# Graph attention over 16 batches: an output tile of its own for batch 14, one key sum on GpSimd, batch 2's labels loaded once, label counts directly behind an eviction

## The chip, the cores and the metric

The kernel runs on one core of a Trainium2 chip. The metric is the device time of one execution in microseconds. Engines are named as in the profile: PE (TensorE matmul), PEld (its weight load), DVE (VectorE), ACT (ScalarE), POOL (GpSimd), SP (the SyncE queue that issues most DMAs).

## The reference

One layer of relation-aware graph attention, with B = 16 batches, N = 512 nodes of F = 512 features, a conditioning vector of 512, H = 16 heads of 32, and keys taken from the first 20 nodes. There are two directions d (the label tensor as it is, and with its node axes swapped). All in float32.

```python
self_feat = concat([v, where(row_zero, 0, q)]) @ W_self.T + b_self
output = self_feat
for d in range(2):
    A = (adj if d == 0 else swapaxes(adj, 1, 2))[:, :, :20, :]      # 11 labels a pair
    mask = A.sum(-1) > 0 ; bias = A @ w_bias + b_bias
    kv = self_feat[:, :20]
    aff = (self_feat Wq[d] + bq) . (kv Wk[d] + bk) / sqrt(32)       # by head
    w = softmax(where(mask, aff, -9e15) + bias)
    output += (w @ kv) @ Wout[d] + bout[d]                          # by head
return v + relu(output)
```

## The kernel before, in words

The order of all instructions is written out by hand; each engine works through its own list in that order, and waits only where a semaphore asks for it.

**Setup.** Keys for all batches are folded into one matrix per batch, so that scores are one product of a batch's features with its "keys". `keys(runs)` does this in 20 bursts (n = 0 to 19): PE fills two PSUM pairs, ACT and DVE evict one half each (L939, L941), and finished blocks are copied by POOL (L945) and sent to DRAM. Bursts 13 to 19 also carry one block product each of batch 0's self features (`block_product`, L284), in the order 1, 2, 6, 7, 5, 4, 3; products 1, 6, 7 and 4 add up in one PSUM bank, `ps_a`, and DVE reads it after each one (`partial`, L297, two instructions). Label work of batch 0's second half lies in these bursts too: `mask_count` (DVE L332: how many labels a pair has, then POOL L333) at n = 15, `mask_sum` (DVE L338: the bias) at n = 17. Both stand behind the block product's DVE instruction in the burst.

**The loop** runs over b = 0 to 14, each pass mixing scores of batch b (seven score products, L397, by a Winograd-like 2x2 scheme), self features of batch b + 1 (`self_product`, L657), softmax of b (`weigh` L522/L523, `expo` L527, `total` L531/L532, `normal` L536 on POOL, `turn` L544) and output of b - 1 and b - 2 (`attend` L567, `finish` L584, `store` L613). The scheme needs sums of key blocks (`key_sum`, L370) and of feature blocks (`feat_sum`, L377 and L384). Key sum 3 of batch 0 is worked out in place, on DVE, ahead of the loop:

```python
        seed_d(0)
        key_sum(0, 3, nc.vector)
        feat_sum(0, 1, nc.vector)
        feat_sum(0, 2, nc.vector)
```

Its reader is score product 7 of batch 0. That product and product 6 share the PSUM tile `ps_a`, which `lowered` (DVE L502) reads between the two. For later batches key sum 3 is on POOL already, one pass ahead.

**Labels.** `load_adj(b, h, ins, ts)` loads half h of a batch's labels (two slices t of 220 KB each; a new buffer of three is taken when slice 0 is among them). `ins` is an instruction behind which the DMA is put in SP's queue. From batch 3 on the four slices come one by one. For batch 2 the code of pass 0 loads slice 0 of half 0, and pass 1 takes new buffers and loads both halves whole; the first slice is thus loaded twice. The labels are read by `mask_mul` (ACT L327, one instruction a label) and `mask_count`.

**The end.** Behind the loop stands a list for b = 15 and o = b - 1 = 14. Outputs are put together in the tile `outt[...]`, tag "o" of the pool `work`, with one buffer: batch 14's tile is batch 13's, whose last two chunks leave by `store(b - 2, range(2, 4))`. Batch 14's output is written by `relieve` (ACT L594: relu out of PSUM), then `residual` (POOL L599: plus x), or by `finish` (DVE L584: both). The first of them stand in this order, where `seed_out` (ACT L554) puts the self features into the PSUM banks of batch 15's output, which `attend(b, ...)` on PE then adds to:

```python
        for q in (3, 2):
            relieve(o, q)
        seed_out(b, 0)
        seed_out(b, 1)
        residual(o, 3)
        total(b, 0, 1)
        normal(b, 0, 1)
        finish(o, 0)
```

Inputs x of batch b lie in four tiles: tags "x0", "x1", "x2" of the pool `load`, and a late tile for b % 4 == 3. "x0" last holds batch 12, whose last reader is `finish(12, ...)` in pass 14.

Of the kernel before, what the change touches and what calls it, by code (L numbers as in the profile page):

```python
# [7 lines left out]
F32 = mybir.dt.float32  # L8
# [10 lines left out]
def gat_kernel(  # L19
# [669 lines left out]
    with tc.tile_pool(name="setup", bufs=1) as sp, tc.tile_pool(name="ps_acc", bufs=4, space=PSUM) as acc["pool"]:  # L689
# [160 lines left out]
        with tc.tile_pool(name="setup_g", bufs=3) as sg:  # L850
# [39 lines left out]
            def value_pieces():  # L890

                while ended:
                    t, ds, ps = ended.pop()
                    rows = min(P, BM - t * P)
                    v = msk.tile([P, H * S], F32, tag="full", name=f"v{t}{ds[0]}")[:, :F]
                    nc.vector.scalar_tensor_tensor(v, br_sb, 0.5, ps, ALU.mult, ALU.add)
                    for i, d in enumerate(ds):
                        edge = EARLY * NG
                        for n, lo, hi in ((0, 0, edge), (1, edge, rows)) if t == 0 else ((1, 0, rows),):
                            nc.gpsimd.dma_start(  # L900
                                vw_d[n][d, :, bass.ds(t * P + lo - n * edge, hi - lo)].rearrange("c r w -> r c w"),
                                v[bass.ds(i * rows + lo, hi - lo)].rearrange("p (c w) -> p c w", c=C),
                            )
# [4 lines left out]
            def keys(runs):  # L908


                pairs = [ps_s.tile([P, 2, 512], F32, tag=f"s{i}", name=f"ps_g{runs[0]}{i}", bufs=1) for i in range(2)]
                at = 0
                for fc, hg, d, lo, hi in runs:
                    n = (hi - lo) * ND
                    for hl in range(HL):
                        r = bass.ts(hl, DH)
                        nc.tensor.matmul(
                            pairs[hl // 2][:, hl % 2, at : at + n], wq_sb[r, d, hg, bass.ts(fc, P)],
                            khD[r, d * C + hg, lo * ND : hi * ND], start=at == 0, stop=True, skip_group_check=True,
                        )  # L920
                    at += n
                if not units and runs is bursts[-1]:
                    for hl in range(HL):
                        r = bass.ts(hl, DH)
                        nc.tensor.matmul(
                            pairs[hl // 2][:, hl % 2, at:], wq_sb[r, 0, 0, :P], khD[r, 0, : 512 - at],
                            start=False, stop=True, skip_group_check=True,
                        )
                at = 0
                for fc, hg, d, lo, hi in runs:  # L930
                    n = (hi - lo) * ND
                    if (fc, hg) not in stages:
                        stages[fc, hg] = (late if hg == C - 1 else sg).tile([P, B, HL, 2, ND], F32, tag="st", name=f"st{fc}{hg}")
                    st = stages[fc, hg]
                    for half in range(2):
                        to = st[:, lo:hi, bass.ts(half, 2), d].rearrange("p b h m -> p h b m")
                        of = pairs[half][:, :, at : at + n].rearrange("p h (b m) -> p h b m", m=ND)
                        if half == 0:
                            nc.scalar.activation(to, of, AF.Copy, scale=SCALE)  # L939
                        else:  # L940
                            nc.vector.tensor_scalar(to, of, SCALE, None, ALU.mult)  # L941
                    at += n
                    if d == 1 and hi == B:
                        to, of = g0[:, fc, bass.ts(hg, WD // C)], st[:, 0].rearrange("p h d m -> p (h d m)")
                        nc.gpsimd.tensor_copy(to, of)  # L945
                        nc.sync.dma_start(g1_d[C * fc + hg], st[:, 1].rearrange("p h d m -> p (h d m)"))
                        if fc * hg < (C - 1) * (C - 1):
                            nc.sync.dma_start(g_d[C * fc + hg], st[:, 2:])
# [40 lines left out]
            for n, runs in enumerate(bursts):  # L989
                for i in range(len(rest)):  # L990
                    if (i < 1 and n > 0) or any(fc == 0 and (d, hg) == rest[0] for fc, hg, d, _, _ in runs):
                        key_rows(*rest.pop(0))
                if n in (3, 4):
                    values(*steps["v"].pop(0)[1])
                if n == 0:
                    bo_rows = load.tile([P, C, N], F32, tag="x2", name="bo_rows", bufs=1)
                    nc.sync.dma_start(bo_rows[:, :2], bout.partition_broadcast(P))
                keys(runs)
                value_pieces()
                if rest:  # L1000
                    for kind in "mm" if n else ():
                        f, args = steps[kind].pop(0)
                        f(*args)
                    continue
                first = n if first is None else first
                for kind in plan[n - first] if n - first < len(plan) else ():
                    f, args = steps[kind].pop(0)
                    f(*args)
                if n == first:
                    for d in range(2):  # L1010
                        nc.gpsimd.tensor_add(br_sb, br_sb, bo_rows[:, d])
                if n > first:
                    value_pieces()
                if n == 7:
                    mask_mul(0, 0)
                if n == 8:
                    mask_count(0, 0)
                if n == 10:
                    mask_sum(0, 0)
                    load_cq(0)  # L1020
                if n == 7:
                    clear_first()
                if n == 9:
                    row_sums(1)
                    copies = blocks(0)
                if n > 13:
                    spill(1, nc.gpsimd)
                    spill(1)
                if n == 11:
                    new_self(0)  # L1030
                    for i in range(1, 5):
                        x_sum(0, i)
                if 10 < n < 15:
                    mask_spread(0, 0, (n - 11,))
                if n == 14:
                    mask_mul(0, 1)
                if n == 15:
                    mask_count(0, 1)
                if n == 16:
                    gs[0] = g0  # L1040
                    key_sum(0, 1)
                    load_adj(1, 0)
                if n == 17:
                    mask_sum(0, 1)
                if n == 18:
                    mask_spread(0, 1)
                    key_bias(0)
                    load_adj(1, 1)
                    load_cq(1)
# [7 lines left out]
    with tc.manual_schedule():  # L1057
        seed_a(0)
        seed_d(0)
        key_sum(0, 3, nc.vector)  # L1060
        feat_sum(0, 1, nc.vector)
        feat_sum(0, 2, nc.vector)
        for b in range(B - 1):
            one, two, more, further = b > 0, b > 1, b + 1 < B, b + 2 < B

            def at(yes, f, *args):
                if yes:
                    f(*args)
# [9 lines left out]
            if b == 1:  # L1078
                self_join(1, 0, 1)
                feat_sum(1, 1)  # L1080
                feat_sum(1, 2)
                total(0, 1, 0)
                normal(0, 1, 0)
                turn(0, 1, 1)
                for h in range(2):
                    load_adj(2, h)
            for q in range(2):
                at(two, finish, b - 2, q)
            at(two, store, b - 2, range(1))
# [44 lines left out]
            if more:  # L1134
                self_join(b + 1, 0, 0)
                feed_c(b + 1)
                self_sum(b + 1, 3)
                mask_mul(b + 1, 0, range(7 if one else 0, 11))
            total(b, 0, 0)
            at(more, load_keys, b + 1, range(2, 3), done["sum"])  # L1140
# [64 lines left out]
            joined_with(b, "c", 1, 0)  # L1205
            if b == 0:
                load_nz(2, done["mixed"])
            at(further, load_adj, b + 2, 0, done["mixed"], slice(0, 1))
            weigh(b, 1, 0)
            at(one, new_outs, b - 1)  # L1210
            at(one, seed_out, b - 1, 2)
# [31 lines left out]
            if more:  # L1243
                if further:
                    seed_a(b + 1)
                    seed_d(b + 1)
                else:
                    full_block(b + 1, 1, 0)
                    seed_block(b + 1, 0, 0, [pair(f"ps_a{b + 1}", b + 1)])
                    seed_block(b + 1, 1, 0, [pair(f"ps_d{b + 1}", b)])  # L1250
                mask_sum(b + 1, 1)
                at(one and further, load_adj, b + 2, 1, done["masks"], slice(1, 2))
                at(b < B - 2, mask_spread, b + 1, 1)
            if b == 0:
# [24 lines left out]
        turn(o, 0, 1)  # L1279
        seed_block(b, 0, 1, [pair("ps_l", 1)])  # L1280
        new_outs(o, ((accs, "c"),))
        seed_out(o, 0)
        seed_out(o, 1)
        load_values(o)
# [112 lines left out]
```

## Time and profile before

| what | us |
|---|---|
| median of 3 runs | 554.29 (554.29 to 554.86) |
| the profiled execution | 554.31 |
| its span, first to last instruction | 552.5 |
| PE busy | 540.7 (98%) |
| PEld busy | 425.3 (77%) |
| DVE busy | 481.1 (87%) |
| POOL busy | 435.9 (79%) |
| ACT busy | 404.2 (73%) |

All times in the rows below are from the start of the span. A row of the timeline has a start, a length, engine, line, operation, what it writes and reads, and a count of merged instructions; in brackets the idle time before it and what ended it. A row of the chain has a start, a length and what. A row of waits has who waited for whom, then total us, times, longest. A row of the windows has the stretch, its length, and the busy time of PE, PEld, DVE, ACT and POOL with instruction counts, then the granted TensorE clock, DMA share and GB/s.

### The profile page before, as it was taken

The page shows a single profiled execution, that of the slowest core. Times are in us where ns is not written, and L with a number is a line of the kernel's source. Part 1 is how long each engine was busy: PE and PEld are TensorE (multiplying, and loading weights), DVE is VectorE, ACT ScalarE, POOL GpSimd, SP SyncE. Part 2 cuts the span into 40 slices and gives each one's busy share as a digit, 9 for nine tenths or more (in the row PEclk, how much of TensorE's full clock was granted, in tenths as well). Part 3 has the DMA queues.
Part 4 walks back from the last instruction along what each step waited for, and adds up shares of the span by engine and source line. Part 5 has one row for each costly group of instructions (what it writes and reads, how often), then busy time and mean ns, then how long its engine had stood idle before and what let it go on. Part 6 is the DMA issues. An engine that isn't in the chain of part 4 may idle for free.

```text
span 552.5 us, 19630 instructions
## 1 busy us (share of the span) xinstructions
PE 540.7 (98%) x7908; PEld 425.3 (77%) x7908; DVE 481.1 (87%) x709; ACT 404.2 (73%) x1000; POOL 435.9 (79%) x420
## 2 busy tenths in 40 slices
PE   9999999999999999999999999999999999999992
PEld 6544368898888878787888888788888787878881
DVE  0776678898989999999999999999999999999985
ACT  1225345788897979888888888888888887877743
POOL 2637896689979797979797888888888889797565
PEclk9999999999999999999999999999999999999998
DMA  8999999958886878788776758686767677654034
GB/s 298 377 396 361 306 355 350 300 188 260 251 254 192 232 223 226 220 224 228 221 217 200 229 178 240 193 234 192 221 197 234 198 222 211 181 146 141 18 100 153
DMA packets 100674, 126.68 MB, mean 229 GB/s; under 512 B 19608, under 2 KB 68822, under 8 KB 98536
## 3 DMA queue, kind: packets, MB, share of 16 engines
q1 hardware_dynamic: 98840, 122.16, 70.7%
q0 software_dynamic: 1168, 2.23, 1.7%
q8 instruction: 62, 1.02, 0.8%
q10 hardware_dynamic: 576, 1.05, 0.5%
q14 instruction: 28, 0.23, 0.2%
HBM read 86.45 MB, written 40.24 MB: 229 GB/s over the span
## 4 chain that ended last, share of the span: by engine, by line
PE 87%; DVE 5%; ACT 2%; POOL 2%; DMA 1%; issue 1%; DVEq 0%; SPq 0%; ACTq 0%; POOLq 0%
PE ps_f L657 29%; PE ps_a L397 21%; PE ps_c L397 11%; PE ps_d L397 5%; PE ps_o_f L567 5%; PE ps_v L883 3%; PE ps_k L825 3%; PE ps_kv L767 1%; PE ps_a L284 1%; PE ps_o_c L567 1%; DMA out_T<-o 1%; POOL w L536 1%; PE ps_c L284 1%; POOL full L440 1%; DMA adj<-in_adj 1%
## 5 line engine op out<-in xcount | busy, mean ns | idle before, releaser
L327 ACT ACTIVATE prod<-adj,wb_sb 128x80 f32<-128x80 int32 x330 | 116.0, 430 | 1.0 <-DMA adj<-in_adj 1.0
L536 POOL TENSOR_TENSOR w<-w,sm 128x640 f32<-128x640 f32 x63 | 80.2, 1273 | 32.6 <-DVE sm L532 31.4
L657 PE MATMUL ps_f<-t,ws_s 128*64 128x246 f32 x720 | 80.0, 370 | 0.0
L657 PEld LDWEIGHTS ps_f<-t,ws_s 128*64 128x64 f32 x720 | 52.2, 136 | 18.5
L527 ACT ACTIVATE w<-w 128x640 f32<-128x640 f32 x60 | 43.9, 732 | 19.3 <-DVE w L523 19.3
L544 DVE STREAM_TRANSPOSE wt<-w 128x640 f32<-128x640 f32 x63 | 52.5, 833 | 2.5 <-POOL w L536 2.4
L657 PE MATMUL ps_f<-x,ws_v 128*64 128x246 f32 x480 | 52.4, 371 | 0.0
L531 DVE TENSOR_REDUCE sm<-w 128x32 f32<-128x640 f32 x63 | 51.1, 811 | 1.0 <-ACT w L527 0.9
L522 DVE TENSOR_REDUCE ps_d<-w 128x32 f32<-128x640 f32 x59 | 48.7, 826 | 1.8 <-ACT ps_d L431 0.2
L523 DVE TENSOR_TENSOR w<-w,ps_d 128x640 f32<-128x640 f32 x59 | 48.4, 821 | 2.0
L657 PEld LDWEIGHTS ps_f<-x,ws_v 128*64 128x64 f32 x480 | 34.7, 137 | 13.0
L370 POOL TENSOR_TENSOR k<-g,k 128x608 f32<-128x608 f32 x30 | 44.6, 1486 | 0.0
L397 PEld LDWEIGHTS ps_a<-g,sf 128*64 128x64 f32 x544 | 34.3, 137 | 5.9 <-issue 5.8
L338 DVE TENSOR_REDUCE add<-prod 128x80 f32<-128x960 f32 x32 | 36.7, 1147 | 2.4 <-POOL prod L333 1.5
L397 PE MATMUL ps_a<-g,sf 128*64 128x152 f32 x544 | 38.6, 295 | 0.0
L397 PE MATMUL ps_d<-g,sf 128*64 128x152 f32 x544 | 37.9, 293 | 0.0
L567 PE MATMUL ps_o_f<-wt,vd 32*32 32x256 f32 (+3 forms) x708 | 37.7, 383 | 0.0
L567 PE MATMUL ps_o_c<-wt,vd 32*32 32x256 f32 (+1 forms) x720 | 36.8, 386 | 0.0
L346 ACT COPY both<-add 64x80 f32<-64x80 f32 x128 | 32.6, 254 | 5.7 <-DVE add L338 4.6
L672 POOL TENSOR_TENSOR t<-x,t 128x492 f32<-128x492 f32 x30 | 34.9, 1163 | 1.2
L397 PEld LDWEIGHTS ps_d<-g,sf 128*64 128x64 f32 x544 | 35.3, 137 | 0.2 <-ACT sf L675 0.2
L333 POOL TENSOR_SCALAR prod<-cond 128x80 f32<-128x80 f32 x32 | 18.0, 563 | 21.6 <-DVE cond L332 20.2
(299 smaller groups left out, 1438.7 us busy)
## 6 DMA issues: line engine op xcount, KB each, us to landing
g<-g_d SPq DMA_DIRECT2D x60, 304.0 KB, 3.6
g_d<-st SPq DMA_DIRECT2D x16, 1064.0 KB, 8.6
out_T<-o SPq DMA_DIRECT2D x63, 256.0 KB, 2.6
x<-in_xT SPq DMA_DIRECT2D x56, 256.0 KB, 4.1
xn<-in_xn SPq DMA_DIRECT2D x48, 256.0 KB
adj<-in_adj SPq DMA_DIRECT2D x53, 220.0 KB, 2.8
vd<-bd_d SPq DMA_DIRECT2D x64, 64.0 KB, 2.3
nz<-nz_d SPq DMA_DIRECT2D x14, 256.0 KB, 4.4
```

Of the source, the lines that this page charges most:

```text
L327: nc.scalar.activation(p[:, :, l], a[:, :, l], AF.Identity, scale=wb_sb[:, l : l + 1])
L338: done["masks"] = nc.vector.tensor_reduce(add, prods.pop((b, h)), AX.X, ALU.add)
L370: done["ksum"] = engine.tensor_sub(to, one, two)
L397: nc.tensor.matmul(slot(g)[bass.ts(p, P // 2), : HL * S].rearrange("p (h m) -> p h m", m=NG)[:, :, 1:], of(k)[:, bass.ds(first + g * P // ...
L522: nc.vector.tensor_reduce(mx, f, AX.X, ALU.max)
L523: done["weigh"] = (engine or nc.vector).tensor_sub(f, f, mx.unsqueeze(2).to_broadcast([P, per, NG]))
L527: done["exp"] = nc.scalar.activation(t, t, AF.Exp)
L531: nc.vector.tensor_reduce(sm, heads(weighs[b, c, l]), AX.X, ALU.add)
L536: done["normal"] = nc.gpsimd.tensor_mul(f, f, smalls.pop((b, c, l)).unsqueeze(2).to_broadcast([P, per, NG]))
L544: done["turn"] = nc.vector.transpose(wts[b][:, c, l], weighs.pop((b, c, l)).rearrange("p g w -> p (g w)"))
L567: nc.tensor.matmul(outsum[b][a][bass.ds(at // 2 * DH, n * DH), bass.ds(c * N // 2 + lo * P, (hi - lo) * P)].rearrange("p (n r) -> p n r", ...
L657: nc.tensor.matmul(parts[b][n in (2, 3, 5)][bass.ts(a, P // 2), bass.ts(i, HN)], lhs, x[:, k], start=False, stop=k == 1, skip_group_check= ...
```

## The change

Four edits. (1) Before batch 14's output is seeded, `outt[14]` is given a tile of its own, tag "x0" of the pool `load`. (2) Key sum 3 of batch 0 leaves its place ahead of the loop on DVE; it is issued on POOL in pass 0, behind `self_sum(1, 3)`. (3) Pass 0 loads both slices of half 0 of batch 2's labels at the place where it loaded one, and half 1 behind `mask_sum(1, 1)`; the two loads of pass 1 go. (4) In the setup, `mask_count(0, 1)` and `mask_sum(0, 1)` move up in their bursts, from the end to directly behind `keys(runs)`.

```diff
                 keys(runs)
+                if n == 15:
+                    mask_count(0, 1)
+                if n == 17:
+                    mask_sum(0, 1)
                 value_pieces()
...
-                if n == 15:
-                    mask_count(0, 1)
...
-                if n == 17:
-                    mask_sum(0, 1)
...
         seed_d(0)
-        key_sum(0, 3, nc.vector)
         feat_sum(0, 1, nc.vector)
...
                 turn(0, 1, 1)
-                for h in range(2):
-                    load_adj(2, h)
...
                 self_sum(b + 1, 3)
+                at(b == 0, key_sum, 0, 3)
                 mask_mul(b + 1, 0, range(7 if one else 0, 11))
...
-            at(further, load_adj, b + 2, 0, done["mixed"], slice(0, 1))
+            at(further, load_adj, b + 2, 0, done["mixed"], slice(0, 1 + (b == 0)))
...
                 mask_sum(b + 1, 1)
+                at(b == 0, load_adj, 2, 1, done["masks"])
...
         new_outs(o, ((accs, "c"),))
+        outt[o] = load.tile([P, C, N], F32, tag="x0", name=f"o{o}", bufs=1)
         seed_out(o, 0)
```

## The prediction

> **What bounds the kernel now.** I read the windows by stage first, then PE's waits, then the timeline at each wait. Times are in us. The span, and the stages:
>
> ```profile
> span 552.5 us, 19630 instructions
> ```
>
> ```profile
> 92.00:103.10 11.10, 10.74 (x140) 8.93 (x136) 10.74 (x12) 6.02 (x14) 8.73 (x8) 1.00 0.91 295
> 103.10:130.00 26.90, 26.55 (x338) 24.03 (x340) 23.47 (x33) 24.14 (x66) 21.87 (x21) 1.00 0.79 259
> ...
> 147.00:490.00 343.00, 343.00 (x5171) 282.72 (x5166) 322.46 (x456) 290.50 (x731) 290.54 (x265) 1.00 0.73 214
> ...
> 535.00:552.50 17.50, 7.82 (x233) 5.98 (x208) 9.40 (x21) 5.98 (x13) 7.81 (x8) 0.87 0.35 128
> ```
>
> The second number is the length, the third PE's busy time. The long middle has no idle PE at all: 343.00 of 343.00. There a microsecond taken from any other engine is worth nothing, and a microsecond gained before it is carried through whole, because PE sets the pace. Only three places are left: some 0.36 before 103.1, 0.35 before 130, and the last 17.5, of which PE works 7.82. PE's waits name them:
>
> ```profile
> PE ps_o_s L567 <- ACT o L594: 2.7, 1, 2.7
> PE ps_o_s L567 <- DVE wt L481: 1.4, 1, 1.4
> ...
> PE ps_a L397 <- DVE w L502: 0.7, 2, 0.4
> ```
>
> The 2.7 is in the end, the 0.7 are the two idle bits of the first passes. Three of the four edits stand at these waits, the fourth stands in the setup. The profiled execution took 554.31, its span 552.5, so 1.81 lie around the span; its time is 0.02 above the median of 554.29, and I work from it. A change of 0.2%, 1.1 us, is about what a measurement of this kernel can tell from none.
>
> **Edit 1, the output tile.** It removes a wait and adds no instruction. The place:
>
> ```profile
> 534.89 0.38 PE L567 MATMUL ps_o_s<-wt,vd 32*32 32x256 f32 x2
> 535.20 4.36 PE L397 MATMUL ps_e<-g,sf 128*64 128x152 f32 x64
> 542.25 0.40 PE L567 MATMUL ps_o_s<-wt,vd 32*32 32x256 f32 x2 [2.70 <-ACT o L594]
> ```
>
> ```profile
> 537.95 1.09 ACT L594 ACTIVATE o<-ps_o_s 128x512 f32<-128x512 f32 x2 [2.57 <-DMA out_T<-o]
> 538.92 1.76 ACT L554 ACTIVATE ps_o_s<-sf 128x512 f32<-128x512 f32 x3
> ```
>
> ```profile
> 537.87 0.69 DVE L584 SCALAR_TENSOR_TENSOR o<-ps_o_c,x 128x512 f32<-128x512 f32 x1 [1.25 <-DMA out_T<-o]
> ```
>
> ```profile
> 533.44 4.26 DMA out_T<-o
> ...
> 538.62 1.26 POOL o L599
> 539.89 1.24 POOL w L536
> 541.15 0.84 DVE wt L544
> ```
>
> PE ends batch 14's `attend` at 534.89 + 0.38 = 535.27. ACT could then take the first `relieve`, but the tile still holds batch 13's chunks, whose store runs from 533.44 to 537.70. ACT idles 2.57, DVE 1.25. Behind the `relieve` everything follows without a gap: ACT 0.6, POOL's `residual` 1.26, POOL's `normal` 1.24, DVE's `turn` 0.84, which ends at 541.99, and PE starts at 542.25. "x0" was last read in pass 14, long ago, so the wait goes and this chain starts 2.57 earlier. What is late next: PE itself, which works on the `ps_e` scores until 535.20 + 4.36 = 539.56; PE would start `attend` at 542.25 - 2.57 = 539.68, just behind. On ACT the three seeds follow the two `relieve`: from 535.38, 1.09 and 1.76 end at 538.2, in time. DVE's `finish` gains its 1.25, starting at 536.62, and its next reader of `ps_e` waits for PE instead. From the `turn` to the last store each step waits for the one before, so the end moves by the same amount; the 1.4 behind L481 stays. Between the bounds 1.25 (DVE's share alone) and 2.69 (542.25 - 539.56, where PE is the limit) I take ACT's row: **-2.57**.
>
> **Edit 2, the key sum.**
>
> ```profile
> 92.06 3.15 DVE L370 TENSOR_TENSOR g<-g 128x608 f32<-128x608 f32 x1
> ...
> 97.72 0.81 DVE L508 TENSOR_TENSOR w<-ps_d,w 128x640 f32<-128x640 f32 x1
> ```
>
> ```profile
> 92.06 1.49 POOL L370 TENSOR_TENSOR k<-g,k 128x608 f32<-128x608 f32 x1
> ...
> 98.89 1.23 POOL L672 TENSOR_TENSOR t<-x 128x492 f32<-128x492 f32 x1
> 102.41 1.27 POOL L536 TENSOR_TENSOR w<-w,sm 128x640 f32<-128x640 f32 x1 [2.28 <-DVE sm L532]
> ```
>
> ```profile
> 100.90 1.83 PE L657 MATMUL ps_f<-t,ws_s 128*64 128x246 f32 x16
> 103.09 2.29 PE L397 MATMUL ps_a<-g,f 128*64 128x152 f32 x32 [0.35 <-DVE w L502]
> ```
>
> ```profile
> 107.44 1.68 PE ps_f L657 x16
> ```
>
> DVE loses an instruction of 3.15; POOL gets one of 1.49, the length of the same operation in its own row. It comes behind the row at 98.89, so from 100.12 to 101.61, into the 2.28 that POOL idles there; `normal` at 102.41 stays clear of it even if it is 0.8 sooner. No DMA moves with it. Its reader, score product 7, now waits for POOL, and at 101.61 PE is still on the run begun at 100.90. That run hands over after 1.68 (the chain's row for such a run), at 102.58; product 7 started at 103.09 because L502 was late. So PE has 0.51 to win and no more, as soon as DVE is 0.5 earlier at L502. Between 0 and -0.51 I take **-0.51**.
>
> How much earlier is DVE? From 92.06 + 3.15 = 95.21 to 97.72 lie the two feature sums, 2.5. Without the key sum they could end at 94.7, 3 sooner. But the same operation takes DVE 3.15 and POOL 1.49, beside each other from 92.06 on. The Trainium skill ("SBUF — State Buffer", Who interferes with whom) has it that a DVE instruction with two SBUF inputs and a GpSimd one that reads SBUF exclude each other for the whole instruction. By that rule, with which the two rows agree, most of the 3.15 was waiting for POOL, and a feature sum will wait in its place. If the first of them then ends only where the key sum ends now, at 95.21, DVE wins one feature sum of two, half of 2.5, instead of 3. L502, which now ends just ahead of 103.09, would still end near 101.9 and ahead of 102.58: the sum is the same by both, with some 0.7 in hand instead of 2.
>
> **Edit 3, the labels.**
>
> ```profile
> 115.50 0.93 SPq L123 DMA_DIRECT2D adj<-in_adj  x1
> ...
> 120.67 0.96 SPq L123 DMA_DIRECT2D adj<-in_adj  x2
> ```
>
> ```profile
> 124.20 1.43 ACT L327 ACTIVATE prod<-adj,wb_sb 128x80 f32<-128x80 int32 x4 [1.04 <-DMA adj<-in_adj]
> ```
>
> ```profile
> 127.90 0.82 DVE L531 TENSOR_REDUCE sm<-w 128x32 f32<-128x640 f32 x1 [0.35 <-ACT w L527]
> ```
>
> ```profile
> 127.72 1.86 PE L657 MATMUL ps_f<-t,ws_s 128*64 128x246 f32 x16
> 129.93 2.29 PE L397 MATMUL ps_a<-g,f 128*64 128x152 f32 x32 [0.35 <-DVE w L502]
> ```
>
> ACT waits 1.04 for labels issued at 120.67. After the change half 0 is issued whole at 115.50, 5.2 earlier, against some 3.5 from issue to use; the 1.04 go. Then ACT's four instructions, three more and the exponential are 1 earlier, DVE's L531 does not wait its 0.35, and DVE's own queue is the limit ahead of L502: it gains 0.35. PE's loss here is 129.93 - (127.72 + 1.68) = 0.53, so 0.35 of it goes: **-0.35**, between 0 and -0.53. On SP's queue one issue of 220 KB goes, and the others move ahead of the next pass's first keys; half 1 waits there for `mask_sum(1, 1)`. Behind it in the queue stand a clear of a DRAM area and the next keys; both are wanted passes later, so nothing on PE waits for them. Buffers rotate one place less, and each is taken over long after its last reader.
>
> **Edit 4, counts and sums.**
>
> ```profile
> 77.45 1.25 DVE L941 TENSOR_SCALAR st<-s_g(3, 0, 0, 0, 16)1_910 128x608 f32<-128x608 f32 x2 [0.59 <-PE s_g(3, 0, 0, 0, 16)1_910 L917]
> 79.07 0.85 DVE L297 SCALAR_TENSOR_TENSOR sf<-nz,qw,ps_a 128x246 f32<-128x246 f32 x2 [0.36 <-PE ps_a L284]
> 79.83 1.06 DVE L332 TENSOR_REDUCE cond<-adj 128x80 f32<-128x880 int32 x1
> 80.81 1.30 DVE L941 TENSOR_SCALAR st<-_g(3, 0, 1, 10, 16)1_940 128x228 f32<-128x228 f32 x3
> ```
>
> ```profile
> 80.07 1.89 PE L284 MATMUL ps_a<-t,ws_s 128*64 128x246 f32 x16
> 81.89 0.65 PE L917 MATMUL s_g(3, 1, 1, 4, 16)0_979<-khD,wq_sb 32*128 32x228 f32 x4
> 82.26 0.46 PE L917 MATMUL s_g(3, 1, 1, 4, 16)1_980<-khD,wq_sb 32*128 32x228 f32 x2
> ```
>
> The count (1.06) goes from behind `partial` to ahead of it: from 78.7 to 79.7, and `partial` from 79.07 to some 79.65, ending near 80.5 instead of 79.92. PE's next block product started at 80.07, right behind it, and adds to the bank that `partial` reads, so it waits: +0.5. Against that the eviction at 80.81 comes 0.2 sooner while PE comes 0.5 later, and the second PSUM pair, which PE began 0.37 behind the first (82.26 against 81.89) because that eviction was late, no longer waits: -0.37. I take **+0.1**, between -0.37 and +0.5. The same trade at n = 17 has one answer: the join that the sum is put ahead of is read two bursts later, and the eviction behind it comes no later than now; nothing.
>
> Whether PE must wait for all of `partial`: DVE's row at 79.07 idled 0.36 until the whole product was done though its first half reads columns written earlier, so the order here is by bank. The Trainium skill ("PSUM — Partial Sum Buffer", PSUM bank collisions raise a hardware error) says to guard a bank by bank and quadrant, not by address. By that rule, with which the trace agrees, the edit costs +0.1; were the order by address, it would bring -0.37, and the sum would be 550.5.
>
> **The sum:** -2.57 - 0.51 - 0.35 + 0.1 = -3.33, and 554.31 - 3.33 = **551.0**.
>
> **The rivals.** (a) The first passes give nothing: DVE stays late at L502 or PE's count stall is paid in full. With only the end, and 0 to +0.5 from the setup: 551.7 to 552.2. For it: small terms, each hanging on one order; against it: POOL and ACT have the slack shown. (b) In the end another wait takes the place, at ACT's seeds or at POOL between `residual` and `normal`, and only DVE's 1.25 comes: 554.31 - 1.25 - 0.76 = 552.3. Against it: both steps follow their releaser without a gap in the chain. (c) The edit does not free the end, because "x0" is still held by something: 553.5, no difference. Against it: its last reader is a pass back. (d) Slower: POOL becomes the bound at score product 7. Each microsecond that the key sum ends after 102.58 is one on PE, and the middle never gives it back. To end above 555.4 it must outweigh 2.57 + 0.35 - 0.1 = 2.82 and 1.1 more against the start at 103.09, so end after 107.0 instead of 101.61, with POOL blocked by DVE again and again. For it: instructions of both engines lengthen each other there already; against it: 5.4 is more than three of them.
>
> **How the numbers follow.** Forecast 0.68 (551.0, own range 550.4 to 551.6), (a) 0.16, (b) 0.07, (c) 0.05, (d) 0.04. Faster is the forecast, (a) and (b): 0.91; same (c) 0.05; slower (d) 0.04. The range reaches up through (a) to 552.2 and down to 550.3, where the setup gives -0.37 and the labels 0.53; that leaves out about 0.16.
>
> **What would show it.** Edit 1: no wait of ACT for `out_T`, the wait of 2.7 gone from PE's list, `turn` about 2.5 earlier against the end of `ps_e`. Edit 2: product 7 right behind its run, POOL's L370 done before it. Edit 3: no wait of ACT for `adj`, PE's idle at the second L502 below 0.2. Edit 4: PE's product of burst 16 some 0.5 later, its burst 17 without the stagger. Wrong it would be if PE showed idle time in the middle, or a new wait between 535 and 542.

## The result, and the profile after

| kernel | median us | lowest to highest | runs | ratio to before, with its 95% interval |
|---|---|---|---|---|
| before | 554.41 | 553.64 to 555.67 | 6 | 1 |
| after | 551.80 | 551.40 to 552.24 | 6 | 0.9951 (0.9938 to 0.9964) |

The change makes the kernel faster by 2.61 us, or 0.5%. The prediction said 551.0, with 550.4 to 551.6 if its likeliest case came true and 550.3 to 552.2 over all. The time lies inside the second range and 0.2 above the first; it also lies inside the 551.7 to 552.2 of rival (a). Measured again in later rounds, after and before stand at 551.96 and 555.52, which is 3.56 apart: before's executions vary more than after's, and the last section tells with what. The profiled execution of after took 552.17, 1.87 more than its span, which the next row gives; the windows of it follow, with the columns as before.

```profile
span 550.3 us, 19621 instructions
```

```profile
92.00:103.30 11.30, 11.30 (x150) 9.72 (x149) 10.18 (x10) 7.22 (x16) 10.87 (x9) 1.00 0.93 306
103.30:129.60 26.30, 26.30 (x338) 22.94 (x335) 23.56 (x33) 23.29 (x63) 20.75 (x20) 1.00 0.78 253
129.60:147.20 17.60, 17.28 (x258) 14.80 (x256) 15.83 (x22) 14.75 (x38) 16.83 (x15) 1.00 0.87 245
147.20:490.00 342.80, 342.80 (x5160) 282.61 (x5152) 322.26 (x456) 290.53 (x731) 290.29 (x265) 1.00 0.74 213
535.00:550.30 15.30, 8.01 (x240) 5.98 (x208) 9.47 (x21) 6.22 (x13) 7.80 (x8) 0.86 0.40 150
```

The idle bits ahead of 103 and 130 are gone: PE works 11.30 of 11.30 and 26.30 of 26.30. The end is 2.2 shorter. But a new idle bit stands where before had none: 17.28 of 17.60 between 129.60 and 147.20. PE's waits in the trace of after, between 141 and 149, give it a name, and the chain of waits of after tells what it hangs on (start, length, what):

```profile
PE ps_o_f L567 <- ACT ps_o_f L554: 0.3, 1, 0.3
```

```profile
142.34 0.83 DVE w L523
...
143.19 0.74 ACT w L527
143.93 0.48 ACT sf L675
144.43 0.61 ACT ps_o_f L554
...
145.09 0.92 PE ps_o_f L567 x3
```

PE waits for ACT's seed of batch 0's output (L554), which stands in ACT's list behind an eviction (L675) and an exponential (L527), and the exponential waits for DVE's `weigh` (L523). For this stretch before's chain is PE from 129.93 on.

The setup's length varies from one execution to the next by itself (last section), so what follows is told in distances between two PE starts of one trace. For before and after:

| from, to | before | after | difference |
|---|---|---|---|
| block product 6, block product 5 (edit 4) | 77.13 to 83.30 = 6.17 | 77.71 to 84.02 = 6.31 | +0.14 |
| first score product, the one of pass 2 (edits 2, 3) | 91.33 to 147.85 = 56.52 | 92.05 to 148.00 = 55.95 | -0.57 |
| from there to the last scores `ps_e` | 147.85 to 535.20 = 387.35 | 148.00 to 535.35 = 387.35 | 0.00 |
| `ps_e`, PE behind its wait for L481 (edit 1) | 535.20 to 545.96 = 10.76 | 535.35 to 543.71 = 8.36 | -2.40 |

From product 5 to the first score product it is 8.03 in both. From L481 to the end of the span lie 6.54 before and 6.59 after, +0.05, which is no more than the rounding of the spans. Product 6 itself starts 0.58 later in after, ahead of everything that the change touches. The sum is +0.58 + 0.14 - 0.57 - 2.40 + 0.05 = -2.20, and the spans differ by 550.3 - 552.5 = -2.2.

### The profile page after: what moved, and what is told of

It reads as the page before. It is cut to its first block, busy times and chain, and to the rows that moved or that the text cites. A ratio compares the mean times of both kernels' runs of the same rounds, so it can differ in the third digit from the quotient of the medians.

```text
span 550.3 us, 19621 instructions
## 1 busy us (share of the span) xinstructions
PE 540.9 (98%) x7908; PEld 424.1 (77%) x7908; DVE 480.0 (87%) x708; ACT 404.4 (73%) x1000; POOL 436.4 (79%) x421
## 4 chain that ended last, share of the span: by engine, by line
PE 92%; DVE 4%; POOL 2%; issue 1%; ACT 0%; DVEq 0%; POOLq 0%; ACTq 0%
PE ps_f L657 30%; PE ps_a L397 23%; PE ps_c L397 11%; PE ps_d L397 6%; PE ps_o_f L567 5%; PE ps_v L883 3%; PE ps_k L825 3%; PE ps_o_c L567 2%; PE ps_kv L767 1%; PE ps_a L284 1%; PE ps_l L397 1%; POOL w L536 1%; PE ps_c L284 1%; PE ps_warm L727 1%; DVE cond L332 1%
## 5 line engine op out<-in xcount | busy, mean ns | idle before, releaser
L527 ACT ACTIVATE w<-w 128x640 f32<-128x640 f32 x60 | 43.8, 730 | 18.5 <-DVE w L523 18.5
L544 DVE STREAM_TRANSPOSE wt<-w 128x640 f32<-128x640 f32 x63 | 52.5, 833 | 1.5 <-POOL w L536 1.4
L523 DVE TENSOR_TENSOR w<-w,ps_d 128x640 f32<-128x640 f32 x59 | 48.4, 821 | 2.0
L333 POOL TENSOR_SCALAR prod<-cond 128x80 f32<-128x80 f32 x32 | 18.0, 564 | 22.1 <-DVE cond L332 20.8
```

The lines of the kernel that those rows point to most:

```text
L523: done["weigh"] = (engine or nc.vector).tensor_sub(f, f, mx.unsqueeze(2).to_broadcast([P, per, NG]))
L527: done["exp"] = nc.scalar.activation(t, t, AF.Exp)
L544: done["turn"] = nc.vector.transpose(wts[b][:, c, l], weighs.pop((b, c, l)).rearrange("p g w -> p (g w)"))
```

## The experiments

### Each edit alone

Four kernels hold one edit each, on top of before; their diffs are those parts of the change's diff. First the output tile:

```diff
+        outt[o] = load.tile([P, C, N], F32, tag="x0", name=f"o{o}", bufs=1)
         seed_out(o, 0)
```

> The kernel before with edit 1 alone (batch 14's output in x0). Theory (sized from the trace of after): the first relieve waits for PE's last result of attend and the signal to ACT, some 0.28 us, not from the moment ACT is free, so the end gains 2.4 us: near 552.0 against 554.4. Rival (the prediction's size, ACT's idle row in full): 2.57. In the trace: ACT L594 from 0.3 after PE's last ps_o_s matmul, PE's wait before the attend of batch 15 0.2 to 0.4 instead of 2.70, everything ahead of 533 as before.

Measured: 551.94 (551.28 to 552.95), ratio 0.9947 (0.9929 to 0.9965). The timeline of this kernel:

```profile
535.19 4.35 PE L397 MATMUL ps_e<-g,sf 128*64 128x152 f32 x64
535.54 1.09 ACT L594 ACTIVATE o<-ps_o_s 128x512 f32<-128x512 f32 x2 [0.16 <-PE ps_o_s L567]
...
539.85 0.41 PE L567 MATMUL ps_o_s<-wt,vd 32*32 32x256 f32 x2 [0.30 <-DVE wt L544]
```

```profile
543.56 0.30 PE L567 MATMUL ps_o_s<-wt,vd 32*32 32x128 f32 x2 [1.40 <-DVE wt L481]
```

From `ps_e` to L481 it is 8.37, as in after: this edit is the whole of the gain in the end. By the times alone it can't be told from the whole change (0.9951).

The key sum:

```diff
-        key_sum(0, 3, nc.vector)
         feat_sum(0, 1, nc.vector)
...
                 self_sum(b + 1, 3)
+                at(b == 0, key_sum, 0, 3)
```

> The kernel before with edit 2 alone (key sum 3 of batch 0 on POOL). Theory: PE's idle time before score product 7 of batch 0 goes and the 0.5 us are carried to the end: near 553.9 against 554.4. Rival: they are given back later as edit 3's gain was, then no difference. In the trace: product 7 at 1.66 behind the start of the run ahead of it, and the same lead at the end of the middle, measured against the burst ahead of the loop.

Measured: 554.67 (552.91 to 555.65), ratio 0.9988 (0.9975 to 1.0001); the first score product of the loop and that of pass 2 start at 91.85 and 147.82, which is 55.97, against 56.52 before. Product 7 of pass 0 follows the start of the run ahead of it by 1.67 (101.42 to 103.09). The 0.55 are carried to pass 2 whole, though PE's wait at the second L502 is 0.51 here and not 0.35. Its one profiled span, 551.1, is short for another reason too (last section).

The labels:

```diff
-                for h in range(2):
-                    load_adj(2, h)
...
-            at(further, load_adj, b + 2, 0, done["mixed"], slice(0, 1))
+            at(further, load_adj, b + 2, 0, done["mixed"], slice(0, 1 + (b == 0)))
...
                 mask_sum(b + 1, 1)
+                at(b == 0, load_adj, 2, 1, done["masks"])
```

> The kernel before with edit 3 alone (batch 2's labels once and sooner). Theory: given back within the pass. PE's wait of 0.35 at the second L502 goes (PE 0.4 earlier at 130), but the chain feature sums on POOL, normal, turn on DVE, weigh, exponential and seed on ACT reaches PE's attend of batch 0 no sooner, so a wait of PE for ACT's L554 of 0.3 to 0.4 appears near 145 and the kernel takes the same time, 554.4 within 0.15. Rival (the prediction): PE carries the gain through, 0.35 to 0.45 faster.

Measured: 555.07 (552.73 to 555.91), ratio 1.0000 (0.9986 to 1.0013). Its timeline:

```profile
129.50 2.29 PE L397 MATMUL ps_a<-g,f 128*64 128x152 f32 x32
130.56 0.84 DVE L544 STREAM_TRANSPOSE wt<-w 128x640 f32<-128x640 f32 x1 [1.21 <-POOL w L536]
```

```profile
144.96 0.92 PE L567 MATMUL ps_o_f<-wt,vd 32*32 32x256 f32 x3 [0.32 <-ACT ps_o_f L554]
```

```profile
147.88 0.61 PE L397 MATMUL ps_a<-g,sf 128*64 128x152 f32 x6
```

PE starts score product 7 of pass 1 at 129.50 instead of 129.93, so the edit wins 0.43 there. But DVE's `turn` (L544) behind it starts at 130.56, against 130.53 in before: it waits for POOL, 1.21 now and 0.75 in before.

```profile
130.53 0.85 DVE L544 STREAM_TRANSPOSE wt<-w 128x640 f32<-128x640 f32 x1 [0.75 <-POOL w L536]
```

By pass 2, which starts at 147.88 against 147.85, everything is given back, and the new wait at 144.96 is where. So it is this edit that goes wrong, and it goes wrong alone too.

The counts and sums:

```diff
                 keys(runs)
+                if n == 15:
+                    mask_count(0, 1)
+                if n == 17:
+                    mask_sum(0, 1)
...
-                if n == 15:
-                    mask_count(0, 1)
...
-                if n == 17:
-                    mask_sum(0, 1)
```

> The kernel before with edit 4 alone (label count and label sum directly behind their evictions). Theory: block product 7 waits for partial, 0.5 us later, and burst 17 loses its stagger, 0.37 sooner, so PE is 0.1 to 0.15 later behind burst 17, and the time 0.1 more at most, under what the rounds can tell. Rival: the stall is not paid back, 0.5 slower; or the order is by address, 0.37 faster. In the trace: distance from the start of block product 6 to that of block product 5 6.3 instead of 6.17.

Measured: 554.93 (553.24 to 556.79), ratio 0.9999 (0.9984 to 1.0014). From product 6 to product 5 it is 77.13 to 83.44 = 6.31, as in after; the stall is this row. Its span is longer by 1.0, of which 0.88 lie behind L481, at a lower clock (last section).

```profile
80.58 1.89 PE L284 MATMUL ps_a<-t,ws_s 128*64 128x246 f32 x16 [0.44 <-DVE sf L297]
```

### What holds the seed back in pass 1

The chain of waits of after, followed back from the seed, leads over DVE to POOL. The timeline of POOL and DVE there:

```profile
121.01 1.28 POOL L377 TENSOR_TENSOR f<-sf 128x512 f32<-128x512 f32 x1 [2.02 <-DVE sf L678]
...
127.08 0.52 POOL L488 TENSOR_TENSOR cqD<-cq 128x160 f32<-128x160 f32 x1
...
127.57 0.62 POOL L628 TENSOR_TENSOR nzD<-nz 128x246 f32<-128x246 f32 x1
...
129.37 1.28 POOL L536 TENSOR_TENSOR w<-w,sm 128x640 f32<-128x640 f32 x1
...
130.69 0.84 DVE L544 STREAM_TRANSPOSE wt<-w 128x640 f32<-128x640 f32 x1 [1.21 <-POOL w L536]
```

POOL idles 2.02 ahead of a feature sum of batch 1 at 121.01 and then works without a gap to the `normal` at 129.37. DVE's `turn` waits for that `normal`, and behind the `turn` stand in DVE's list the evictions, the label count (which POOL's L333 and, behind it, L499 wait for) and the `weigh` that the exponential waits for. The theory: two short POOL instructions, `key_bias` (L488) and `flag_difference` (L628), stand in the busy part; put into the idle gap, they free 1.1 us of POOL there, and the seed comes in time. Then edit 3 is worth its 0.4 to 0.5. The rival: the seed is late for DVE's own queue, and POOL's order changes nothing. The edit on top of after is this; a second kernel has it with edit 3 undone:

```diff
             if b == 1:
+                key_bias(1)
+                flag_difference(2)
                 self_join(1, 0, 1)
...
-            at(one, key_bias, b)
+            at(two, key_bias, b)
...
-            at(more, flag_difference, b + 1)
+            at(more and b != 1, flag_difference, b + 1)
```

> The kernel after, and in pass 1 alone key_bias(1) and flag_difference(2) (0.53 and 0.62 on POOL) go ahead of feat_sum(1, 1), into the 2.0 us that POOL idles there. Theory: what gave edit 3's gain back is the chain that starts at POOL's feat_sum(1, 1) and ends at ACT's seed of batch 0's output; shortened by some 1 us it is no longer the limit, so PE's wait for ACT's L554 near 145 goes and PE keeps the 0.45: the attend of batch 0 and all behind it 0.4 sooner than in after, measured from the first score product of the loop (55.95 to the score product at 148.00 becomes 55.5). Near 551.4. Rival: the seed waits for something else (its own ACT order, the transposed weights), and the distance stays 55.95.

Measured: 550.86 (550.49 to 551.43), ratio 0.9924 (0.9909 to 0.9940). Its timeline:

```profile
118.53 0.54 POOL L488 TENSOR_TENSOR cqD<-cq 128x160 f32<-128x160 f32 x1
119.01 0.63 POOL L628 TENSOR_TENSOR nzD<-nz 128x246 f32<-128x246 f32 x1
120.59 1.28 POOL L377 TENSOR_TENSOR f<-sf 128x512 f32<-128x512 f32 x1 [0.95 <-DVE sf L678]
```

```profile
91.62 0.87 PE L397 MATMUL ps_a<-g,sf 128*64 128x152 f32 x10
```

```profile
146.67 1.90 PE L397 MATMUL ps_a<-g,sf 128*64 128x152 f32 x26
```

The two instructions lie in the gap, PE's wait for L554 is gone from its list (the weight load's is down to 0.2 from 1.0), and from loop start to pass 2 it is 55.05, 0.90 less than in after: the rival falls. But 0.90 is twice the 0.45 that the theory had; the next kernel shows why.

> The same move with edit 3 undone (batch 2's labels as in the kernel before). Theory: the labels then hold the second L502 as before, and PE has nothing to keep: distance 55.9 to 56.0, as in after, 0.4 longer than with the labels sooner. Rival: the move on POOL alone brings the 0.4 (then edit 3 is worth nothing with it either).

Measured: 551.23 (550.99 to 552.38), ratio 0.9933 (0.9919 to 0.9948), and a distance of 55.53 (91.44 to 146.97). So the move alone brings 0.42, without edit 3. I had expected 55.9 to 56.0 here; the rival was right in this part: before already had the loss that the move removes. The four distances together, each with edit 2 in it:

| | edit 3 out | edit 3 in |
|---|---|---|
| POOL's order as it was | 55.97 | 55.95 |
| the two instructions in the gap | 55.53 | 55.05 |

Without edit 2 the upper line reads 56.52 (before) and 56.55 (labels alone). Edit 3 is worth nothing while POOL's order is as it was, and 0.48 once it is mended.

That the chain behind the `turn` sets the start of pass 2 can be read from the traces of five kernels, counted from the first score product of the loop:

| | `turn` (L544) of pass 1 | pass 2 | between |
|---|---|---|---|
| before | 130.53 - 91.33 = 39.20 | 56.52 | 17.32 |
| edit 2 alone | 130.50 - 91.85 = 38.65 | 55.97 | 17.32 |
| edit 3 alone | 130.56 - 91.33 = 39.23 | 56.55 | 17.32 |
| after | 130.69 - 92.05 = 38.64 | 55.95 | 17.31 |
| after, with the two instructions in the gap | 129.20 - 91.62 = 37.58 | 55.05 | 17.47 |

In the first four, pass 2 comes 17.31 or 17.32 behind that `turn`, wherever PE stood at product 7. Edit 2 stands ahead of the chain and moves the `turn` by 0.55; edit 3 does not move it. With the two instructions in the gap the `turn` no longer waits, and the chain is no longer what pass 2 waits for.

The loss in before can be read in its own trace, but not where the prediction looked. Three views of before: the windows, PE's waits between 141 and 149, and the chain.

```profile
130.00:147.00 17.00, 17.00 (x256) 14.72 (x256) 15.78 (x22) 14.46 (x37) 16.23 (x15) 1.00 0.78 237
```

```profile
PEld ps_o_f L567 <- ACT ps_o_f L554: 0.5, 2, 0.3
```

```profile
143.00 2.07 PE ps_a L397 x32
145.07 0.78 PE ps_o_f L567 x3
...
147.92 1.18 PE ps_a L397 x15
```

PE counts as busy for all 17.00. Yet the weight load waits 0.5 for the seed, and the chain needs 4.92 from the start of this score product, over `attend`, to the next pass (143.00 to 147.92), where the same in the next pass takes 4.46, from 172.11 to 176.57:

```profile
172.11 2.07 PE ps_a L397 x32
174.18 0.33 PE ps_o_f L567 x2
...
176.57 1.44 PE ps_a L397 x19
```

The first matmuls of `attend` are on record as begun and as lasting longer, 0.78 where the next pass has 0.33, so the wait counts as work. The Trainium skill ("Perfetto Trace Analysis", Identifying the Most-Contended Engine) says that matmul busy time is a poor measure of how near a kernel is to its limit, and points to the weight loads' share instead. This trace agrees: PE counts as busy for 4.92 of 4.92 in this stretch and for 4.46 of 4.46 in the next pass, the weight loads for 3.17 (64%) and 3.04 (68%). In a longer stretch their share alone would not have shown the loss: 14.72 of 17.00 in before, and 14.47 of 17.00 with the two instructions in the gap, where the wait is gone.

### The count one burst later, and all of it together

```diff
-                if n == 15:
+                if n == 16:
                     mask_count(0, 1)
```

> The kernel after with the label count behind the eviction of burst 16 instead of 15. Theory: partial of burst 15 is not held up, so block product 7 starts without its wait of 0.44, and the eviction of burst 16 starts as soon as PE is done, so burst 17 has no stagger either: from block product 6 to block product 5 5.8 instead of 6.31 (before: 6.17), and all behind it 0.5 sooner. Rival: the count now holds up partial of burst 16 or the eviction of burst 17 and the 0.5 comes back there.

Measured: 551.21 (550.77 to 551.98), ratio 0.9932 (0.9918 to 0.9946). From product 6 to product 5 it is 77.18 to 82.98 = 5.80, against 6.31 in after and 6.17 in before. The count ahead of `partial` is what the stall came from. One burst later it costs nothing that these distances show: it then holds up the read of product 7, and the product behind that, 5, goes to another bank (`ps_c`) and starts without a wait.

The last version has the POOL move, the count at 16, and in the end `normal` ahead of `residual`:

```diff
-        residual(o, 3)
         total(b, 0, 1)
         normal(b, 0, 1)
+        residual(o, 3)
```

> The kernel after with the POOL move, the count at burst 16, and at the end normal(15, 0, 1) ahead of residual(14, 3) on POOL. Theory: 0.4 and 0.5 add up, and turn of batch 15 is some 0.2 sooner, so PE's 0.30 ahead of its attend goes: 1.1 below after, near 550.7. Rival: the end keeps its length because residual(14, 3) and the stores behind it are then late.

Measured: 550.16 (549.66 to 551.25), ratio 0.9914 (0.9899 to 0.9930). From product 6 to 5 5.80, from loop start to pass 2 55.04 (91.90 to 146.94), and from `ps_e` to L481 8.31. The swap in the end brought 0.05 and not the 0.2 expected: PE's wait of 0.30 ahead of `attend` is gone, but its wait for L481 grows by as much, to 1.67 from 1.36. By these distances the version gains 1.48 on after, more than the 1.1 expected, since the POOL move brings 0.9 and not 0.4.

Two last kernels, after and this version side by side:

> The kernel after itself, on the chip and in the rounds of the next one. Theory: 551.8 within 0.6, and the distances of its first profile again within 0.05: from the first score product to that of pass 2 55.95, from the ps_e scores to the last attend 8.36, whatever the length of the setup in this execution. Rival: the distances differ by as much as the setups do, and then they cannot carry the argument.

> The kernel with the two moves and the swap, beside after on one chip. Theory: 1.4 to 1.6 faster than after (0.9 in pass 1, 0.5 in the setup, 0.05 at the end): 550.2 to 550.5. Rival: most of it was the chip of the other call, then within 0.5 of after.

Measured: after 551.96 (551.16 to 552.51), ratio 0.9942 (0.9923 to 0.9962); the version with all of it 550.40 (549.82 to 551.11), ratio 0.9917 (0.9897 to 0.9936). It is 1.56 below after, by its terms 0.51 + 0.91 + 0.06 = 1.48 (6.31 - 5.80, 55.95 - 55.04, 8.36 - 8.30).

## Why the prediction was right, and where not

**Edit 1: the mechanism as told, -2.40 instead of -2.57.** In after, ACT's `relieve` waits for PE and no longer for the store:

```profile
535.04 0.38 PE L567 MATMUL ps_o_s<-wt,vd 32*32 32x256 f32 x2
...
535.35 4.36 PE L397 MATMUL ps_e<-g,sf 128*64 128x152 f32 x64
...
535.70 1.08 ACT L594 ACTIVATE o<-ps_o_s 128x512 f32<-128x512 f32 x2 [0.16 <-PE ps_o_s L567]
...
536.66 1.76 ACT L554 ACTIVATE ps_o_s<-sf 128x512 f32<-128x512 f32 x3
...
540.01 0.41 PE L567 MATMUL ps_o_s<-wt,vd 32*32 32x256 f32 x2 [0.30 <-DVE wt L544]
```

The mis-sized term is the row that it took: ACT's idle time of 2.57 began at 535.38, when ACT was free, and not when PE's result could reach it. PE's last matmul of batch 14's `attend` ends at 535.04 + 0.38 = 535.42 in after, and ACT starts 0.28 behind that. In before that end is 535.27, so ACT could start at 535.55 at the earliest, 0.17 behind the start of its idle time. From 535.27 to the old start at 537.95 are 2.68; less 0.28 they make 2.40, the number measured. The seeds and `residual` came in time, so rival (b) fell, and with "x0" free rival (c) fell too.

**Edit 2: -0.55 instead of -0.51, by the way that the rule of the Trainium skill had.** The timeline of after:

```profile
92.86 3.00 DVE L377 TENSOR_TENSOR f<-sf 128x512 f32<-128x512 f32 x1
...
95.89 1.52 DVE L384 TENSOR_TENSOR f<-f,sf 128x512 f32<-128x512 f32 x1
...
97.34 0.81 DVE L508 TENSOR_TENSOR w<-ps_d,w 128x640 f32<-128x640 f32 x1
...
100.30 1.48 POOL L370 TENSOR_TENSOR g<-g 128x608 f32<-128x608 f32 x1
...
103.28 0.94 PE L397 MATMUL ps_a<-g,f 128*64 128x152 f32 x12
```

In before the first of these had taken half as long:

```profile
95.14 1.63 DVE L377 TENSOR_TENSOR f<-sf 128x512 f32<-128x512 f32 x1
```

An instruction of 3.15 left DVE, but L508 starts only 0.38 sooner, 1.10 sooner against the loop's start, which is 0.72 later in this execution. The feature sum L377 now takes the 3.00 instead of 1.63. The Trainium skill ("SBUF — State Buffer", Who interferes with whom) says that a DVE instruction with two inputs there and a GpSimd one that reads there exclude each other; the run agrees, with the wait moved from one such instruction to the next. No run here holds POOL still beside DVE, so the rule itself is not tested. The 1.10 were enough. POOL's key sum ends at 101.78, where 101.61 was forecast, product 7 starts with no wait, and rival (d) was far off.

**Edit 3: nothing instead of -0.35. This is the step that failed.** Its local part held: ACT's wait for the labels went, and with this edit alone PE's product 7 of pass 1 came 0.43 earlier, more than the 0.35. What failed is the sentence "a microsecond gained before it is carried through whole, because PE sets the pace". The row behind it began at 147.00. Between 130 and 147, which it left out, PE counts as busy throughout but already waited 0.46 for ACT's seed, through its weight loads, on a chain of POOL, DVE and ACT that the edit does not shorten. A PE that comes earlier waits longer there. Edit 2's 0.55 came through because they moved the start of that chain too, and not because PE sets the pace. Of rival (a), "the first passes give nothing", this half came true, for another reason than a late DVE at L502 or a stall paid in full; the other half, edit 2, did not.

**Edit 4: +0.14 instead of +0.1, in both its parts.** The timeline of after:

```profile
79.19 1.06 DVE L332 TENSOR_REDUCE cond<-adj 128x80 f32<-128x880 int32 x1
...
80.17 0.84 DVE L297 SCALAR_TENSOR_TENSOR sf<-nz,qw,ps_a 128x246 f32<-128x246 f32 x2
...
81.16 1.89 PE L284 MATMUL ps_a<-t,ws_s 128*64 128x246 f32 x16 [0.44 <-DVE sf L297]
```

From product 6 to 7 it is 3.45 instead of 2.94, +0.51; from 7 to 5 2.86 instead of 3.23, -0.37, as the second PSUM pair no longer lags. PE did wait for the read of its bank, and the forecast by bank held. The sum moved at n = 17 cost nothing, as forecast: the 8.03 from product 5 to the loop are as before.

**The sum.** By distances -2.40 - 0.55 + 0 + 0.14 = -2.81 where -3.33 was forecast: 0.35 of the difference is edit 3 and 0.17 edit 1. The medians differ by 2.61 in the first rounds and by 3.56 in the last, one below the sum by distances and one above. So the times alone do not tell the forecast from rival (a), and that the median fell into the range given over all owes something to the rounds.

## What to carry to other kernels

A gain ahead of a stretch with "no idle time" is carried through only if every wait in that stretch has room: compare the same stage between two passes, and read what the weight loads wait for, because a stalled matmul can count as busy. Where a gain vanishes, follow the chain from the new wait back to the first idle gap of another engine; the mending was there, two short instructions moved into 2 us that POOL idled. And for the start of an idle time that an edit removes, take the moment when the result of the next releaser has arrived (here 0.28 behind its end), not when the engine fell free.

## What the runs showed that I had not expected

**The store that held the end varied.** The same transfer, of the same tile and at the same place, took 4.26 in before, but in the kernel with the key sum alone:

```profile
533.40 2.88 DMA out_T<-o
```

```profile
540.85 0.41 PE L567 MATMUL ps_o_s<-wt,vd 32*32 32x256 f32 x2 [1.32 <-ACT o L594]
```

PE's wait was then 1.32 instead of 2.70, and from `ps_e` to L481 it was 9.39 instead of 10.76. With the 0.55 of edit 2 and a loop that began 0.52 later, that is the span of 551.1: -1.37 - 0.55 + 0.52 = -1.40 against 552.5. So edit 1 removes a wait that is itself not constant; before's runs lie between 552.64 and 556.33 over all comparisons, after's between 551.16 and 552.51. Part of this spread goes with the clock, as follows; the store's part in it was not tested.

**The clock after that wait.** The windows of the kernel with counts and sums alone, and of before, which waited as long there (2.65 and 2.70):

```profile
544.00:546.00 2.00, 1.60 (x61) 0.65 (x48) 1.90 (x5) 0.37 (x2) 0.87 (x1) 0.50 0.51 184
546.00:548.00 2.00, 1.81 (x48) 0.93 (x48) 0.02 (x1) 0.49 (x3) 1.40 (x2) 0.50 0.58 218
```

```profile
544.00:546.00 2.00, 0.59 (x46) 0.32 (x41) 1.80 (x5) 0.68 (x3) 1.56 (x3) 1.00 0.51 182
546.00:548.00 2.00, 0.92 (x48) 0.48 (x48) 0.94 (x3) 0.38 (x1) 1.20 (x2) 1.00 0.79 297
```

The granted clock was 0.50 in the one and 1.00 in the other, and the last PE work took 1.81 instead of 0.92; hence the span of 553.5. The Trainium skill ("TensorE: Matmul & The Clock Gate", The HAM clock gate) has the clock at half after an idle window of some 3.4 us, and the window run freely, so that the moment of a change depends on its phase. That the two executions differ fits; the pause here was shorter than that figure.

One profile of each does not show whether the wait brought the lower clock, but each run's mean granted clock over its span is known, and it divides the kernels:

| kernels | runs | of them with a clock of 0.993 or less |
|---|---|---|
| before, and edits 2, 3 and 4 each alone | 87 | 51 |
| edit 1 alone | 6 | 0 |
| all others with edit 1 | 41 | 0 |

The lowest clock with edit 1 is 0.994. Of before's 51 runs in this table, the 30 at the lower clock took 555.64 in the mean and the other 21 took 554.27, or 1.37 less. So edit 1 does a second thing that the prediction did not have: with it the longer executions at a lower clock do not appear. No distance in the table of before and after shows this, since both profiles lie at 0.996. How many of before's runs were at the lower clock sways its median: in the last rounds, with the 3.56, they were 7 of 11; for the first, with the 2.61, their clocks are not on record. A lower clock under PE's work is shown by one profile only, the one above, and no run changes the length of the wait by itself.

**The setup's own spread.** Block product 6, ahead of every edit, starts between 76.90 and 78.07 in the profiled executions. Terms of 0.1 to 0.5 us can't be read from spans or single times of this kernel; distances inside a trace repeat to a few hundredths (55.95 and 55.97 for after, 55.04 twice for the last version).
